# Joint attention stage of a decoder kernel: which scores share a buffer, and where the row maxima are joined

## Chip, cores and metric

One core of one Trainium2 chip runs the whole program. The metric is the device time of one execution in microseconds (us). The chip's engines are TensorE (PE; its weight loads are listed apart as PEld), VectorE (DVE), ScalarE (ACT), GpSimd (POOL) and SyncE (SP), which issues the DMAs.

## What is computed

The reference is a two-layer decoder on 16 x 128 = 2048 rows of 256 features. Each layer has a self-attention, a cross-attention and a feed-forward network, each followed by a layer norm on the sum with its input. The change lies in layer 0's cross-attention, which has 16 heads of 16 dimensions and fake-quantised operands and weights; its 2048 queries see 2048 keys:

```python
q = jnp.transpose((x @ Wq + bq) * scale, ...)      # per head
q = _fq_sym(q, axis=-1)      # round(q / s) * s with s = max|q| / 127
k = _fq_sym(k, axis=-1)
v = _fq_sym(v, axis=2)
attn = jnp.einsum('bhqd,bhkd->bhqk', q, k)
attn = jax.nn.softmax(attn.astype(jnp.float32), axis=-1)
attn = _fq_unsigned(attn, axis=-1)     # round(a / s) * s with s = max(a) / 255
out = jnp.einsum('bhqk,bhkd->bhqd', attn, v)
return out @ Wp + bp
```

The layer norm and layer 0's feed-forward network (silu(gate) * up, then down, 1024 wide) follow. Since the largest softmax weight of a row is exp(0) over the sum, the quantised weight is round(255 * exp(score - max)): the kernel writes exp(score - max + ln 255) as an 8-bit integer, and needs for it the maximum over all 2048 keys of a row.

## The kernel before, in words

The program runs layer 0's self-attention, then the joint stage (L0 cross-attention together with L0's feed-forward network), then layer 1. Only the joint stage is touched.

**Steps.** A step is one tile of 128 queries (`u` of a pair `gp` of tiles) and one pair of heads (`i`): 8 pairs of tiles x 8 pairs of heads x 2 tiles = 128 steps, n = 0 to 127. Sixteen steps that share `gp` are called a group here; they are numbered r0 to r15 in it. A step has two parts, `part` 0 and 1, and `at = 2 * n + part`. Nine more steps at the end drain the pipeline.

**Scores** (`scores`, L781; matmuls at L788). A score buffer `s` has 2 x 512 float32 columns[...], and there are two such buffers. A part takes two of them. Keys and queries are held with 64 rows a head (48 of them in use: three bfloat16 parts of 16 dimensions), so the two heads of a pair lie on rows 0 to 63 and 64 to 127. Before the change a buffer holds the same 512 keys of both heads; the quarters of the 2048 keys come in order.

**Scaling** (`scaled`, L791; L795). One DVE instruction a head and quarter multiplies 128 x 512 scores by the query's scale `qs` into the tile `e` in SBUF and takes the maximum along the row. From the second quarter on it begins with the maximum so far (a second scalar operand, `smx`), so that the fourth quarter's maximum is that of the row. `e` has four buffers, two a step.

**Exponent and weights** (`exponent`, L808; L810 and `weights8`, L812; L819). ACT turns the two maxima of a step into `snl` = ln 255 - max, and a step later takes exp(e + snl) of 128 x 2048 elements to 8 bits, once for each head.

**Turning and spreading** (`words_T`, L828; `words_out`, L834; `spread`, L840). PE transposes the 8-bit weights as 32-bit words, four 128 x 128 blocks into a PSUM tile `aTp` (L831). A copy takes it to SBUF (`at`, L837): in part 0 on DVE, in part 1 on ACT. POOL widens it to bfloat16 (L841). Then PE multiplies with the values (`context`, L854), 32 output rows a head.

**Order.** The scheduler keeps the written order on PE, DVE, ACT and POOL (`manual_schedule`). Work with no place of its own goes through `later(at, engine, f)` and `due(at, engine)`: queries of the next pair of tiles, the division by the softmax sums (L882), the output projection (L887, L890), norm statistics (L136, L137), and the feed-forward network: a `unit` (L922 matmuls; L940 tanh and L941 copy on ACT; L944, L947 and L948 on POOL) in r0, r1, r2, r9, r11, r12, r14 and r15, from the second group on, and its down projection (L957) in r3 to r5 from the third. In every part PE's order is: score buffer 1 of the part, some context, the transposes, score buffer 0 of the next part, more context, feed-forward.

Of the kernel before, what the change touches and what calls it, by code (L numbers as in the profile page):

```python
# [18 lines left out]
F32 = mybir.dt.float32  # L19
# [3 lines left out]
AF = mybir.ActivationFunctionType  # L23
ALU = mybir.AluOpType
AX = mybir.AxisListType
PSUM = bass.MemoryType.PSUM

P = 128
# [4 lines left out]
G = 512  # L33
# [15 lines left out]
def decoder(ctx: ExitStack, tc: tile.TileContext, w: dict, out: bass.AP):  # L49
    nc = tc.nc  # L50

    const = ctx.enter_context(tc.tile_pool(name="const", bufs=1))
    stat = ctx.enter_context(tc.tile_pool(name="stat", bufs=4))
# [156 lines left out]
    with ExitStack() as ph:  # L210
        pool = ph.enter_context(tc.tile_pool(name="l0a", bufs=1))
# [12 lines left out]
        wts, bias = {}, {}  # L224
        for hg in range(4):
            cols = slice(hg * G, (hg + 1) * G)
            for nm in ("Wlk", "Wq", "Wlv"):
                t = wts[nm, hg] = pool.tile([P, 2, G], F32, name=f"{nm}_{hg}")
# [8 lines left out]
            t = wts["Wo", hg] = pool.tile([P, 4, HID], F32, name=f"Wo_{hg}")  # L237
# [284 lines left out]
        states, cks = {}, {}  # L522
# [4 lines left out]
        with tc.manual_schedule(engines={mybir.EngineType.PE}):  # L527
# [4 lines left out]
            for n in range(len(steps) + 6):  # L532
# [34 lines left out]
                g, r = (n + 10) // 16, (n + 10) % 16  # L567
# [21 lines left out]
    with ExitStack() as ph:  # L589
# [173 lines left out]
        nc.sync.dma_start(out=wp2, in_=w["L0_xattn_Wp"].rearrange("(c p) n -> p c n", p=P))  # L763
        for c in range(2):
            nc.gpsimd.tensor_scalar(wp2[:, c], wp2[:, c], sv[:, c : c + 1], 1.0, ALU.mult, ALU.mult)
        ln255 = pool.tile([P, 1], F32, name="ln255")
        nc.gpsimd.memset(ln255, math.log(255.0))

        wk = ph.enter_context(tc.tile_pool(name="l0x_k", bufs=2))
        ps = ph.enter_context(tc.tile_pool(name="l0x_ps", bufs=1, space=PSUM))  # L770
# [7 lines left out]
            ssum = stat.tile([P, 2, 16], F32, tag="ssum", name="ssum", bufs=3)  # L778
            groups[gp] = ([], ssum)

        def scores(gp, i, u, half, c):  # L781

            t = 2 * gp + u
            s = ps.tile([P, 2, G], F32, tag="s", name="s", bufs=2)
            at = (2 * half + c) * G
            for hh in range(2):
                r = slice(64 * hh, 64 * hh + 64)
                nc.tensor.matmul(s[:, hh, :], lhsT=qT[t % 4][r, i, :], rhs=kT[r, i, at : at + G], start=True, stop=True)  # L788
            return s

        def scaled(gp, i, u, half, c, st, s):  # L791

            quarter = 2 * half + c
            for hh in range(2):
                nc.vector.tensor_scalar(  # L795
                    st["e"][hh][:, half, c * G : (c + 1) * G],
                    s[:, hh, :],
                    qs[2 * gp + u][:, 2 * i + hh : 2 * i + hh + 1],
                    None if quarter == 0 else st["mx"][:, quarter - 1, hh : hh + 1],
                    ALU.mult,  # L800
                    ALU.max,
                    accum_out=st["mx"][:, quarter, hh : hh + 1],
                )

        def head(i, hh):
            return 4 * (i // 2) + i % 2 + 2 * hh

        def exponent(st):  # L808
            st["nm"] = stat.tile([P, 2], F32, tag="snl", name="snl")
            nc.scalar.activation(st["nm"], st["mx"][:, 3, :], AF.Identity, bias=ln255, scale=-1.0)  # L810

        def weights8(gp, i, u, hh, st):  # L812

# [20 lines left out]
        def words_out(hh, st, pt, copy):  # L834

            at = wk.tile([P, 4, P], F32, tag="at", name="at", bufs=3)
            copy(at.bitcast(U16), pt.bitcast(U16))  # L837
            st["at"][hh] = at
# [137 lines left out]
        def due(at, engine):  # L976
            for f, args in put_off.pop((at, engine), []):
                f(*args)
# [135 lines left out]
        with tc.manual_schedule(engines=set(ordered)):  # L1114
            for n in range(len(steps) + 9):
                now = steps[n] if n < len(steps) else None
                if now is not None:
                    if n % 16 == 0:
                        group(n // 16)
                    if n < NB:  # L1120
                        nc.gpsimd.tensor_tensor(xs[n], xs[n], bp, ALU.add)
                    states[n] = {
                        "e": [wk.tile([P, 2, 2 * G], F32, tag="e", name="e", bufs=4) for _ in range(2)],
                        "mx": stat.tile([P, 4, 2], F32, tag="smx", name="smx"),
                        "a": [],
                        "at": {},
                    }
                for part in range(2):
                    at = 2 * n + part
                    if now is not None:  # L1130
                        if at == 0:
                            waiting = scores(*now, 0, 0)
                        scaled(*now, part, 0, states[n], waiting)
                        scaled(*now, part, 1, states[n], scores(*now, part, 1))
                    due(at, "DVE")
                    m = n - 2 + part
                    due(at, "PE")
                    for hh in range(2):

                        q = n - 3 if (n - 3) % 2 == 1 else n - 4  # L1140
                        turn = (2 * (n - q) + part, hh)

                        if hh == 1 and 0 <= m < len(steps):
                            pt = words_T(1 - part, states[m])
                        if hh == 1 and at + 1 < 2 * len(steps):
                            waiting = scores(*steps[(at + 1) // 2], (at + 1) % 2, 0)
                        if 0 <= q < len(steps) and turn in turns:
                            gp, i, _ = steps[q]
                            if turn == (7, 0) and i % 4 == 0:
                                os[gp, i // 4] = ps.tile([P, 2 * P], F32, tag="o", name="o")  # L1150
                            o = os[gp, i // 4]
                            context(i, range(*turns[turn]), aTs[gp, i], o)
                            if turn == (9, 1):
                                aTs.pop((gp, i))
                                if i % 4 == 3:
                                    later(
                                        at + 1,
                                        "ACT first",
                                        nc.scalar.copy,
                                        ot[:, i // 4],  # L1160
                                        os.pop((gp, i // 4)).rearrange("p (u q) -> p u q", u=2),
                                    )
                                if i == 7 and gp < LAST:
                                    later(at, "DVE last", sums, gp)
                                    for u in range(2):
                                        later(at + 1, "POOL", by_dim, gp, u)
                    if part == 1:
                        unit(n, 1, at)
                    due(at, "ACT first")

                    if 0 <= n - 1 < len(steps):
                        weights8(*steps[n - 1], part, states[n - 1])
                    if 0 <= m < len(steps):
                        words_out(1 - part, states[m], pt, nc.scalar.copy if part else nc.vector.tensor_copy)
                    due(at, "ACT")
                    if 0 <= n - 2 < len(steps):
                        gp, i, u = steps[n - 2]
                        if part == 0 and u == 0:
                            aTs[gp, i] = wk.tile([P, NB, 2, 2 * P], BF16, tag="aT", name="aT")
                        due(at, "POOL first")  # L1180
                        spread(u, part, states[n - 2], aTs[gp, i])
                    due(at, "POOL first")
                    due(at, "POOL")
                    if now is not None and part == 1:
                        exponent(states[n])
                    due(at, "DVE last")
                    if (n, part) == (len(steps), 1):
                        later(at + 1, "DVE", sums, LAST)
                        for u in range(2):
                            later(at + 2, "POOL", by_dim, LAST, u)  # L1190
                    if n < len(steps):
                        pair_work(n, bool(part))
                    else:
                        tail_work(n, bool(part))
                if n == len(steps) + 3:
                    ffn_load_all()
                states.pop(n - 3, None)
            assert not put_off, put_off

            for i in range(NI):  # L1200
                for n in range(2):
                    ffn_gate(LAST, i, n, "s")
                th, gu = ffn_tiles(LAST, i, tail=True)
                ffn_out(LAST, th, gu)
                ffn_sigmoid(th, nc.vector)
                ffn_mult(LAST, i, th, gu, nc.vector)
            exp_tables()
            for u in range(2):
                ffn_put_out(LAST, range(NI * u, NI * u + NI), 0, "s")
                due(1, "DVE")  # L1210
            due(1, "POOL")
            due(2, "POOL first")
# [498 lines left out]
```

## Time and profile before

| what | value |
|---|---|
| median of 3 runs | 2860.21 us (2859.89 to 2861.86) |
| profiled execution, its own time | 2860.04 us |
| its span, first to last instruction | 2858.3 us |
| joint stage, first to last scaling (L795) | 879.6 to 1750.0 us |
| busy, whole span | PE 2607.9, DVE 2071.4, ACT 1584.7, POOL 1238.4 us |
| busy, 880 to 1750 us | DVE 854, PE 740, ACT 732, POOL 638 us |
| mean granted PE clock | 0.962 |

How to read it: the profile lists for each engine the instructions with their start and length. A group's line gives the source line, the engine, the operation, output and inputs by the program's names and shapes, the count, then the busy time, the mean length in ns, and the idle time of that engine just before them with what ended it. A window's line gives the stretch, its length, the busy time (and count of instructions) of PE, PEld, DVE, ACT and POOL, the granted clock of PE, the DMA share and GB/s. Busy lengths of neighbouring instructions overlap, so what an instruction costs its engine is read from start to start in the timeline.

### The profile page before, as it was taken

The page shows a single profiled execution, that of the slowest core. Times are in us where ns is not written, and L with a number is a line of the kernel's source. Part 1 is how long each engine was busy: PE and PEld are TensorE (multiplying, and loading weights), DVE is VectorE, ACT ScalarE, POOL GpSimd, SP SyncE. Part 2 cuts the span into 40 slices and gives each one's busy share as a digit, 9 for nine tenths or more (in the row PEclk, how much of TensorE's full clock was granted, in tenths as well). Part 3 has the DMA queues.
Part 4 walks back from the last instruction along what each step waited for, and adds up shares of the span by engine and source line. Part 5 has one row for each costly group of instructions (what it writes and reads, how often), then busy time and mean ns, then how long its engine had stood idle before and what let it go on. Part 6 is the DMA issues. An engine that isn't in the chain of part 4 may idle for free. (4 is left out here: it accounts for less than half of the span.)

```text
span 2858.3 us, 44732 instructions
## 1 busy us (share of the span) xinstructions
PE 2607.9 (91%) x15989; PEld 1620.2 (57%) x16020; DVE 2071.4 (72%) x5525; ACT 1584.7 (55%) x2858; POOL 1238.4 (43%) x1390
## 2 busy tenths in 40 slices
PE   6999999999976788888889888899988899999998
PEld 3677777777753344444445444566655555665646
DVE  5677877877759999999999995577877763233232
ACT  3455555555536888878888885455555442222120
POOL 5644544444446667768777776323322200000000
PEclk9999999999996889999999999999999999999999
DMA  8000000000010000000000001400010012111120
GB/s 239 2 1 1 1 1 1 1 1 1 1 38 10 1 12 20 25 12 25 23 12 27 19 16 50 145 2 1 2 49 12 6 38 67 36 53 48 41 62 13
DMA packets 85006, 79.69 MB, mean 28 GB/s; under 512 B 19728, under 2 KB 66288, under 8 KB 84272
## 3 DMA queue, kind: packets, MB, share of 16 engines
q1 hardware_dynamic: 83520, 73.41, 8.5%
q0 software_dynamic: 1264, 3.42, 0.5%
q8 instruction: 127, 2.08, 0.3%
q14 instruction: 95, 0.78, 0.1%
HBM read 74.57 MB, written 2.23 MB: 27 GB/s over the span
## 5 line engine op out<-in xcount | busy, mean ns | idle before, releaser
L795 DVE TENSOR_SCALAR_CACHE_REDUCE e<-s,qs,smx 128x512 f32<-128x512 f32 x768 | 581.5, 806 | 12.3 <-PE s L788 11.7
L841 POOL CAST aT<-at 128x2048 bf16<-128x2048 uint8 x256 | 482.9, 1891 | 194.7 <-DVE at L837 133.4
L819 ACT ACTIVATE a<-e,snl 128x2048 uint8<-128x2048 f32 x256 | 510.8, 1998 | 2.8
L788 PE MATMUL s<-kT,qT 64*128 64x512 bf16 x1024 | 216.4, 416 | 99.6 <-DVE e L795 97.1
L1623 DVE TENSOR_TENSOR h<-h,up 128x512 f32<-128x512 f32 (+1 forms) x100 | 68.8, 688 | 192.6 <-PE up L1619 191.3
L854 PE MATMUL o<-aT,vq 128*32 128x256 bf16 x2048 | 193.7, 294 | 0.0
L831 PE MATMUL aTp<-ident,a 128*128 128x128 f32 x1024 | 181.7, 304 | 13.0 <-ACT a L819 12.6
L788 PEld LDWEIGHTS <-qT 64*128 64x128 bf16 x1024 | 61.9, 94 | 228.6 <-issue 227.5
L795 DVE TENSOR_SCALAR_CACHE_REDUCE e<-s,qs 128x512 f32<-128x512 f32 x256 | 179.6, 739 | 4.8 <-PE s L788 4.8
L1622 ACT ACTIVATE h<-gate 128x512 f32<-128x512 f32 (+1 forms) x100 | 59.7, 597 | 220.5 <-PE gate L1619 220.3
L1619 PE MATMUL gate<-xT,w_L_ffn_w1g 128*128 128x512 f32 x352 | 167.7, 595 | 0.0
L837 ACT COPY at<-aTp 128x1024 uint16<-128x1024 uint16 x128 | 128.4, 1003 | 69.6 <-PE aTp L831 64.7
L1619 PE MATMUL up<-xT,w_L_ffn_w1u 128*128 128x512 f32 x352 | 165.4, 592 | 0.0
L1333 DVE TENSOR_REDUCE amx<-sc 128x8 f32<-128x1024 f32 x96 | 116.7, 1215 | 62.2 <-PE sc L1324 62.0
L831 PEld LDWEIGHTS aTp<-ident,a 128*128 128x128 f32 x1024 | 116.6, 150 | 77.2 <-issue 35.8
L1650 PE MATMUL py<-w_L_ffn_w2T,h 128*128 128x256 f32 x704 | 154.6, 379 | 0.0
L1336 ACT ACTIVATE pr<-pr 128x1024 f32<-128x1024 f32 x96 | 101.6, 1059 | 88.3 <-DVE pr L1335 88.3
L1345 ACT COPY prT<-tp 128x512 f32<-128x512 f32 x192 | 104.2, 583 | 76.8 <-PE tp L1344 76.4
L1650 PEld LDWEIGHTS py<-w_L_ffn_w2T,h 128*128 128x128 f32 x704 | 133.7, 190 | 18.3
L922 PE MATMUL gu<-xT,wgu 128*128 128x256 f32 x448 | 128.4, 410 | 1.8 <-ACT gu_s L941 1.7
L854 PEld LDWEIGHTS <-vq 128*32 128x32 bf16 x2048 | 72.7, 98 | 100.0 <-issue 94.5
L443 ACT ACTIVATE pls<-sc,lm,rms_rs 128x128 f32<-128x128 f32 x256 | 113.7, 453 | 21.7 <-DVE lm L439 21.7
(319 smaller groups left out, 5961.7 us busy)
## 6 DMA issues: line engine op xcount, KB each, us to landing
wgu<-in_L_ffn_gu SPq DMA_DIRECT2D x112, 128.0 KB
sh<-share SPq DMA_DIRECT2D x32, 256.0 KB
sh<-share SPq DMA_DIRECT2D x16, 224.0 KB
sh<-share SPq DMA_DIRECT2D x16, 192.0 KB
w_L_ffn_w1g<-in_L_ffn_w1g SPq DMA_DIRECT2D x1, 2816.0 KB
w_L_ffn_w1u<-in_L_ffn_w1u SPq DMA_DIRECT2D x1, 2816.0 KB
w_L_ffn_w2T<-in_L_ffn_w2T SPq DMA_DIRECT2D x1, 2816.0 KB
sh<-share SPq DMA_DIRECT2D x16, 160.0 KB
```

What stands on the lines that cost most here:

```text
L443: nc.scalar.activation(pls[:, h, :], by_head[:, h // 2, h % 2, NC4:NK], AF.Exp, bias=nm[:, h : h + 1], scale=rq[:, h : h + 1], accum_out=s ...
L788: nc.tensor.matmul(s[:, hh, :], lhsT=qT[t % 4][r, i, :], rhs=kT[r, i, at : at + G], start=True, stop=True)
L795: nc.vector.tensor_scalar(st["e"][hh][:, half, c * G : (c + 1) * G], s[:, hh, :], qs[2 * gp + u][:, 2 * i + hh : 2 * i + hh + 1], None if ...
L819: nc.scalar.activation(a.bitcast(U8), st["e"][hh].rearrange("p a b -> p (a b)"), AF.Exp, bias=st["nm"][:, hh : hh + 1], accum_out=groups[g ...
L831: nc.tensor.transpose(pt[:, b, :], st["a"][hh][:, b * P : (b + 1) * P], ident)
L837: copy(at.bitcast(U16), pt.bitcast(U16))
L841: nc.gpsimd.tensor_copy(aT[:, :, hh, u * P : (u + 1) * P].rearrange("p (b j) q -> p b j q", j=4), st["at"].pop(hh).bitcast(U8).rearrange(" ...
L854: nc.tensor.matmul(o[r : r + 32], lhsT=vq[:, n, h // 2, h % 2 : h % 2 + 2].rearrange("p w d -> p (w d)"), rhs=aT[:, n, hh], start=n == 0 a ...
L922: nc.tensor.matmul(ffn_ps[q][:, n, :], lhsT=wt[:, k, :], rhs=xT[q // 2][:, k, at], start=k == 0, stop=k == 1)
L1333: nc.vector.tensor_reduce(mx, sc, AX.X, ALU.max)
L1619: nc.tensor.matmul(pp[:rows], lhsT=wt[:, k, :], rhs=xT[g][:, k, :], start=k == 0, stop=k == 1)
L1650: nc.tensor.matmul(py, lhsT=h[:rows, i4 * P : (i4 + 1) * P], rhs=wt, start=n == 0, stop=n == len(parts) - 1)
```

## The change

Three things change. First, in the first half of a step (part 0, keys 0 to 1023) a score buffer holds one head's 1024 keys in place of both heads' 512, and one DVE instruction scales all 1024; in the second half both heads share a buffer as before. Second, no scaling begins with an earlier maximum: a step leaves three maxima a head, which DVE joins at the end of the step with a reduction, and DVE also forms ln 255 - max, which ACT did; this comes right behind the last scaling in the order. Third, the copy of transposed words is on DVE only in part 0 of even steps (`at % 4 == 0`), otherwise on ACT.

```diff
-        ln255 = pool.tile([P, 1], F32, name="ln255")
-        nc.gpsimd.memset(ln255, math.log(255.0))
...
-        def scores(gp, i, u, half, c):
+        def scores(gp, i, u, half, x):
             t = 2 * gp + u
             s = ps.tile([P, 2, G], F32, tag="s", name="s", bufs=2)
-            at = (2 * half + c) * G
-            for hh in range(2):
+            for j in range(2):
+                hh, c = (x, j) if half == 0 else (j, 2 + x)
                 r = slice(64 * hh, 64 * hh + 64)
-                nc.tensor.matmul(s[:, hh, :], lhsT=qT[t % 4][r, i, :], rhs=kT[r, i, at : at + G], start=True, stop=True)
+                nc.tensor.matmul(
+                    s[:, j, :], lhsT=qT[t % 4][r, i, :], rhs=kT[r, i, c * G : (c + 1) * G], start=True, stop=True
+                )
             return s
-        def scaled(gp, i, u, half, c, st, s):
-            quarter = 2 * half + c
-            for hh in range(2):
+        def scaled(gp, i, u, half, x, st, s):
+            blocks = [(x, s.rearrange("p a b -> p (a b)"), st["e"][x][:, 0, :])]
+            if half == 1:
+                blocks = [(hh, s[:, hh, :], st["e"][hh][:, 1, x * G : (x + 1) * G]) for hh in range(2)]
+            for hh, src, dst in blocks:
                 nc.vector.tensor_scalar(
-                    st["e"][hh][:, half, c * G : (c + 1) * G],
-                    s[:, hh, :],
+                    dst,
+                    src,
                     qs[2 * gp + u][:, 2 * i + hh : 2 * i + hh + 1],
-                    None if quarter == 0 else st["mx"][:, quarter - 1, hh : hh + 1],
+                    None,
                     ALU.mult,
                     ALU.max,
-                    accum_out=st["mx"][:, quarter, hh : hh + 1],
+                    accum_out=st["mx"][:, half + half * x, hh : hh + 1],
                 )
         def exponent(st):
+            m = stat.tile([P, 2], F32, tag="smm", name="smm")
+            nc.vector.tensor_reduce(m, st["mx"].rearrange("p q h -> p h q"), AX.X, ALU.max)
             st["nm"] = stat.tile([P, 2], F32, tag="snl", name="snl")
-            nc.scalar.activation(st["nm"], st["mx"][:, 3, :], AF.Identity, bias=ln255, scale=-1.0)
+            nc.vector.tensor_scalar(st["nm"], m, -1.0, math.log(255.0), ALU.mult, ALU.add)
...
-                        "mx": stat.tile([P, 4, 2], F32, tag="smx", name="smx"),
+                        "mx": stat.tile([P, 3, 2], F32, tag="smx", name="smx"),
...
                         scaled(*now, part, 1, states[n], scores(*now, part, 1))
+                        if part == 1:
+                            exponent(states[n])
...
-                        words_out(1 - part, states[m], pt, nc.scalar.copy if part else nc.vector.tensor_copy)
+                        words_out(1 - part, states[m], pt, nc.vector.tensor_copy if at % 4 == 0 else nc.scalar.copy)
...
-                    if now is not None and part == 1:
-                        exponent(states[n])
```

## The prediction

> **What bounds the kernel now.** I read the 40 slices first (VectorE, DVE, at 9 tenths only where line 795 runs), then the costliest groups, then the windows of the joint stage, step by step. The stage's 128 steps run from 879.6 us (first instruction of L795) to 1750.0 us (its last): 870 of the 2858.3 us span. Eight groups of 16 steps take 103, 107, 111, 110, 109, 110, 111 and 109 us. Everything that the change touches lies there.
>
> The costliest groups, columns as on the page (count, then busy us, mean ns, idle before):
>
> ```profile
> L795 DVE TENSOR_SCALAR_CACHE_REDUCE e<-s,qs,smx 128x512 f32<-128x512 f32 x768 | 581.5, 806 | 12.3 <-PE s L788 11.7
> L788 PE MATMUL s<-kT,qT 64*128 64x512 bf16 x1024 | 216.4, 416 | 99.6 <-DVE e L795 97.1
> L795 DVE TENSOR_SCALAR_CACHE_REDUCE e<-s,qs 128x512 f32<-128x512 f32 x256 | 179.6, 739 | 4.8 <-PE s L788 4.8
> L837 DVE COPY at<-aTp 128x1024 uint16<-128x1024 uint16 x128 | 87.6, 684 | 1.3 <-PE aTp L831 1.3
> ```
>
> DVE hardly ever waits for scores (16.5 us in 870); TensorE (PE) waits 97 us for DVE to free a score buffer. So DVE sets the pace. But by how much? The windows of the fourth group, one per step (us, then busy PE, PEld, DVE, ACT, POOL, then PE clock), show it; I number its steps r0 to r15:
>
> ```profile
> 1206.72:1213.06 6.34, 6.34 (x46) 3.44 (x47) 6.34 (x18) 6.31 (x11) 5.47 (x6) 1.00 0.16 44
> ...
> 1241.09:1248.02 6.93, 4.21 (x31) 1.94 (x29) 6.93 (x18) 4.80 (x5) 6.50 (x9) 0.84 0.00 0
> 1248.02:1257.67 9.65, 9.09 (x52) 4.64 (x50) 8.31 (x26) 6.27 (x8) 3.27 (x2) 0.76 0.01 3
> 1257.67:1264.01 6.34, 3.88 (x23) 1.68 (x22) 6.34 (x19) 4.39 (x5) 5.90 (x8) 0.64 0.00 0
> 1264.01:1270.95 6.94, 6.94 (x49) 3.51 (x46) 6.42 (x20) 5.77 (x8) 3.89 (x3) 0.84 0.07 19
> ...
> sum 110.31, PE 97.06 PEld 52.45 DVE 107.94 ACT 93.39 POOL 84.00; mean PE 6.07 PEld 3.28 DVE 6.75 ACT 5.84 POOL 5.25
> ```
>
> DVE is busy 107.9 of 110.3 us, but r1 (first row) has PE and ACT full as well, and in r7 and r9 PE, at half clock for part of the time, already makes the step longer than DVE's busy time. The bound is DVE's by a small margin in the odd steps and by a large one in r6, r8 and r14.
>
> PE in r1, back to back (start us, length, what):
>
> ```profile
> 1207.63 0.39 PE L788 MATMUL s<-kT,qT 64*128 64x512 bf16 x2
> 1207.95 0.39 PE L854 MATMUL o<-aT,vq 128*32 128x256 bf16 x4
> 1208.28 0.66 PE L831 MATMUL aTp<-ident,a 128*128 128x128 f32 x4
> 1208.86 0.39 PE L788 MATMUL s<-kT,qT 64*128 64x512 bf16 x2
> 1209.18 0.51 PE L854 MATMUL o<-aT,vq 128*32 128x256 bf16 x6
> 1209.62 1.13 PE L922 MATMUL gu<-xT,wgu 128*128 128x256 f32 x4
> ```
>
> Both score matmuls of a buffer end within 0.39 us, no longer than one alone: they lie on different halves of the array's rows and run together (starts 4 ns apart). The next step's first score starts at 1213.73: PE needs 6.10 us for a step to which DVE gives 6.34.
>
> **The change, part by part.** DVE first. From its timeline, start to start: a scaling instruction with only the query scale takes 0.67 us, one that also takes the running maximum 0.73, the copy 0.61. A step is 2 x 0.67 + 6 x 0.73 + 0.61 = 6.33, the 6.34 of the plain windows.
>
> After, a step has two scalings of 1024 and four of 512, all without the running maximum. 512 more elements cost 0.53 us (the reductions of 128x512 and 128x1024 take 683 and 1215 ns), so a long one takes 1.20 start to start. The copy stays in even steps only. The join X: the last accumulator read and its wait about 0.12 (83 ns, plus the 35 ns that each dependent DVE pair here shows), the reduction 0.17 (rnm 169 ns; np_mv, six in and two out, 182), 35 ns, then 0.08 start to start for the small scalar operation (sums, L469). X = 0.40; at least 0.25 (the reduction of svs took 102), at most 0.55. It runs in DVE's queue ahead of the postponed work and the next step's first scaling, which wait that long; it can't gain. Even step: 2 x 1.20 + 4 x 0.67 + 0.61 + 0.40 = 6.09, 0.24 less. Odd: 5.48, 0.85 less. Mean 0.55, over 128 steps 70 us of DVE time.
>
> Here a rule speaks against the saving. The Trainium skill, VectorE: DVE Perf Modes, "The DRAIN you can't avoid", says that a semaphore between DVE operations costs nothing extra, since the pipe empties anyway. Six of the eight scalings now wait for an earlier maximum. By the rule they would save nothing by losing that, and the mean saving would be 0.55 - 6 x 0.063 = 0.17 us, 22 us in all. The rows show 0.73 against 0.67 for equal tiles (whether the wait or the second scalar operand costs it, they don't tell); the change takes both away, so I take the rows.
>
> PE: in the first half of a step a buffer's two matmuls are now of one head, on the same rows, so they follow each other. Pairs of o matmuls follow at 0.11 for 256 columns, so 512 take 0.21; the weight load hides behind the first matmul, as in the gu chain (0.22 apart). Two buffers a step: +0.43 us at full clock, +0.85 at half; at least zero (they can't overlap better than now), at most 0.62 if the second load (94 ns) isn't hidden. The skill's TensorE: Matmul & The Clock Gate, "Back-to-back issue gap", gives about 131 ns a matmul for a load-matmul stream at 512 columns, by which the cost would be 0.26; nothing here runs that fast, so 0.43. It lies on the path wherever PE has no slack.
>
> ACT: the 128 snl operations leave (0.34 each, start to start), 64 copies come (1.0 each, 0.9 start to start): even steps -0.34, odd +0.56, so its 93.4 us become about 95. The copy in odd first halves waits on PE's transposes between two exponentials, so the second exponential and whatever needs it slip 0.9 us; the tiles e of scaled scores are two steps deep, which covers it while ACT is under about 2 us late. The maximum now comes 0.4 us after the last scaling, as it did through ACT (0.37). The memset that goes, POOL's spreads and SP's weight loads keep their cost and place: nothing.
>
> **The sum.** For the fourth group, DVE per step after: 6.1, 5.5, 6.1, 5.7, 7.0, 6.6, 6.7, 7.5, 6.1, 5.6, 6.9, 5.6, 6.0, 6.3, 6.3, 5.4, together 99.2 (its busy time less 0.24 or 0.85). PE's work per step, by its timeline from score to score less its idle, was 5.5, 6.1, 5.6, 6.5, 6.4, 7.5, 4.2, 8.7, 4.5, 7.0, 5.6, 5.7, 6.2, 6.2, 4.7, 6.7; with 0.43 added (0.7 in r7, r8 and r9, partly at half clock): 6.0, 6.5, 6.0, 7.0, 6.8, 7.9, 4.6, 9.4, 5.2, 7.7, 6.0, 6.2, 6.6, 6.6, 5.1, 7.1, together 104.7. The larger of the two in each step adds up to 110.1. After r6, r8 and r14 PE enters a buffer ahead, about 0.8 each: -2.4. PE's short waits for ACT and DVE (4.6 us in this group: 1.9 for exponentials, the rest for x, qa, rows) now partly lie in steps that PE bounds: +2. PE is denser in r6 to r8, so I take off a third of the 3.4 us that the half clock costs r7 and r9: -1.1. That leaves about 108.6 to 109.3: a gain of 1 us a group, 6 in groups three to eight. The first group has no feed-forward work; DVE gains 0.24 and 0.85 in turn and PE at half clock gives back some 2.5 us: -6. The second is like it up to r8: -3.5. In all -15.5 against the profiled run's 2860.04 (span 2858.3), which is 0.2 us from the median of 2860.21: **2845**. The gain of 70 goes mostly to PE, which is late next in every odd step.
>
> **The rivals.** PE hides its extra: if the half clock vanishes with the denser PE, or most stalls do, DVE's full 70 us come through: 2790, halfway 2810. For it: r6, r8 and r14 have slack. Against it: r1's full PE row. Chance 0.12.
>
> Slower: PE's extra matmuls fall on steps without slack. Credit for lead gone, waits for exponentials doubled (ACT has 6.3 of 6.34 in r1 to r3 and more copies), half clock as now: 110.1 + 2 + 1.5 = 113.6 a group, less 0.7 of smoothing, 112.9: +2.6, six times, less 9.5: +6, so 2866; with unhidden loads (0.19 more a step, 3 us a group) up to 2880. It decides once PE's work and waits pass 110.3 a group, that is from 0.4 us of unhidden stalls a step. Chance 0.28.
>
> Break-even: both meet within 0.2% (5.7 us, about what a measurement of this kernel can tell from no change): 2857. Chance 0.16. That the change doesn't do what it says I exclude: the instruction order of the built kernel has two long and four short scalings, a reduction and a scalar operation each step.
>
> **How the numbers follow.** The likeliest case, 2828 to 2854, holds 0.44; with the first rival faster is 0.54 (a little of the case ends above 2854.5), same 0.17, slower 0.29. The range reaches 2816 to 2872.
>
> **What would show it.** Long scalings at 1.20 start to start, short ones at 0.67, X at 0.4; score pairs of first halves 0.6 us long; DVE's waits for scores up from 16 us to over 60; PE's for DVE down from 97 to under 60; odd steps at about 6.5 with PE full, even at 6.1. I am wrong if DVE stays full (then near 2790), or if PE waits for ACT's exponentials over 0.5 us a step (then slower).

## The result, and the profile after

The changed kernel takes 2922.58 us (median of 4 runs, 2921.71 to 2922.69) against 2860.05 (4 runs, 2857.31 to 2861.86): 62.5 us longer, ratio 1.022 [1.020, 1.024]. The profiled execution took 2921.71 us, its span is 2920.0. The joint stage, first to last scaling, grew from 870.4 to 926.3 us; the other 6 us of the span lie before and behind it. The groups of 16 steps went from 103, 107, 111, 110, 109, 110, 111 and 109 us to 107, 109, 118, 120, 120, 120, 120 and 115.

The costliest groups of the changed kernel, the ones that answer to those shown of before (count, busy us, mean ns, idle before and who ended it):

```profile
L798 DVE TENSOR_SCALAR_CACHE_REDUCE e<-s,qs 128x512 f32<-128x512 f32 (+1 forms) x768 | 674.3, 921 | 82.2 <-PE s L787 80.3
L824 ACT ACTIVATE a<-e,snl 128x2048 uint8<-128x2048 f32 x256 | 513.4, 2010 | 55.9 <-DVE snl L815 55.6
L787 PE MATMUL s<-kT,qT 64*128 64x512 bf16 x1024 | 280.6, 422 | 74.5 <-DVE e L798 71.0
```

DVE's scalings fell from 761 busy us to 678 (each the sum of its two groups), and DVE now waits 80 us for scores where it waited 16.5: so far as foretold. But in the middle line ACT's exponentials wait 55.6 us for `snl`, the operand that DVE now makes. Before, ACT made `snl` itself and waited there for DVE's maxima:

```profile
ACT snl L810 <- DVE e L795: 33.2, 34, 6.8
```

So that wait is not new, but it is 22 us longer. The groups of DVE in the joint stage, each shape apart, say why:

```profile
L798 DVE TENSOR_SCALAR_CACHE_REDUCE e<-s,qs 128x512 f32<-128x512 f32 x512 | 356.8, 746 | 32.0 <-PE s L787 31.5
L798 DVE TENSOR_SCALAR_CACHE_REDUCE e<-s,qs 128x1024 f32<-128x1024 f32 x256 | 321.2, 1273 | 50.2 <-PE s L787 48.8 <-ACT at L842 0.4
L815 DVE TENSOR_SCALAR snl<-smm 128x2 f32<-128x2 f32 x128 | 74.8, 584 | 4.5
...
L813 DVE TENSOR_REDUCE smm<-smx 128x2 f32<-128x6 f32 x128 | 20.4, 159 | 4.4
```

The reduction of six maxima to two takes 159 ns. The scalar operation behind it, on two elements a row, takes 584 ns on average, 74.8 us in all. The line for its tile gives shortest, median and longest:

```profile
L815 DVE TENSOR_SCALAR snl<-smm x128: 169/458/1887, 887.2 to 1808.3; 128x2 f32<-128x2 f32 x128
```

An operation whose size is fixed and whose time goes from 169 to 1887 ns is waiting inside. For what, two timelines show, of DVE and then of POOL, between r6 and r7 of the fourth group (start us, length us):

```profile
1267.89 0.16 DVE L813 TENSOR_REDUCE smm<-smx 128x2 f32<-128x6 f32 x1
1268.09 1.73 DVE L815 TENSOR_SCALAR snl<-smm 128x2 f32<-128x2 f32 x1
1269.73 1.27 DVE L798 TENSOR_SCALAR_CACHE_REDUCE e<-s,qs 128x1024 f32<-128x1024 f32 x1
```

```profile
1264.23 5.56 POOL L846 CAST aT<-at 128x2048 bf16<-128x2048 uint8 x3
```

POOL's third cast ends at 1264.23 + 5.56 = 1269.79; the scalar operation ends at 1269.82. Over all 128: the 39 that start with POOL idle take 169 to 172 ns, every one. Of the 61 that start during a cast (918 ns on average) 55 end 21 to 25 ns after that cast's end; of the 28 that start during other POOL work (L952, L953, L1126) 22 end 23 to 26 ns after its end. The remaining twelve started in the last 82 ns of POOL's instruction and took 169 to 172 ns, as with POOL idle. All 128 wait for one semaphore, which only DVE sets, so the program ties none of them to POOL; the operation holds DVE's queue, with the next step's first scaling behind it, until POOL's instruction is over. The Trainium skill, SBUF — State Buffer, "SBUF: two separate sides", has a rule of this shape: DVE and GpSimd share a port pair, which a DVE instruction in a two-port mode takes as an exclusive lock, and the loser blocks fully. VectorE: DVE Perf Modes, "The perf-mode tier table", lists a float32 `tensor_scalar` in SBUF in such a mode, but reductions and float32 operations that read PSUM not. The numbers agree: the scalings read PSUM and the reduction is a reduction, and neither waited (158 to 161 ns for every one of the 128 reductions).

The kernel before shows the same outside the joint stage. A plain scalar operation on 128x256 from SBUF to SBUF (L719) takes 293 ns with POOL idle and 495 to 726 in the 13 cases that start while POOL runs; the reductions of L385 stay at 623 to 689 whether POOL runs or not. Operations on two SBUF tiles (L293) stretch too: 409 to 417 ns with POOL idle, up to 1106 otherwise.

The second part shows in PE's timeline of r1, the step the prediction took as its example:

```profile
1221.25 0.60 PE L787 MATMUL s<-kT,qT 64*128 64x512 bf16 x2
1221.78 0.50 PE L859 MATMUL o<-aT,vq 128*32 128x256 bf16 x6
...
1223.28 0.60 PE L787 MATMUL s<-kT,qT 64*128 64x512 bf16 x2
...
1224.73 0.39 PE L787 MATMUL s<-kT,qT 64*128 64x512 bf16 x2
1225.05 0.51 PE L859 MATMUL o<-aT,vq 128*32 128x256 bf16 x6
...
1227.78 0.60 PE L787 MATMUL s<-kT,qT 64*128 64x512 bf16 x2
```

A pair of score matmuls of one head takes 0.60 us, a pair of two heads 0.39 as before, and r1 lasts 6.53 us from its first score to the next step's, as was worked out (6.10 + 0.43). The windows of the fourth group (r1, r4, r6, r7 and the sum; us, then busy PE, PEld, DVE, ACT, POOL, then PE clock):

```profile
1222.76:1229.09 6.33, 6.33 (x45) 3.09 (x44) 5.93 (x16) 6.33 (x9) 4.15 (x4) 1.00 0.16 45
...
1241.98:1251.59 9.61, 7.13 (x41) 4.04 (x41) 8.67 (x20) 6.83 (x8) 7.46 (x7) 0.97 0.01 2
...
1261.48:1269.73 8.25, 6.26 (x43) 3.04 (x42) 8.18 (x18) 4.27 (x5) 7.80 (x9) 1.00 0.01 2
1269.73:1277.20 7.47, 5.71 (x40) 2.84 (x39) 7.26 (x21) 6.82 (x7) 1.96 (x2) 1.00 0.00 0
...
sum 119.52, PE 105.46 PEld 53.23 DVE 106.14 ACT 97.05 POOL 83.57; mean PE 6.59 PEld 3.33 DVE 6.63 ACT 6.07 POOL 5.22
```

r1 (6.33 from scaling to scaling) has PE full, as foretold. r4 and r6 have an operation of 1.89 and 1.73 us in them; in r6 DVE is full for that reason, and POOL nearly so. DVE's busy time, foretold as 99.2, is 106.1, and no engine is full over the group's 119.5 us.

### The profile page after: what moved, and what is told of

Read it like the earlier page. It is cut to its first block, busy times and chain, and to the rows that moved or that the text cites. A ratio compares the mean times of both kernels' runs of the same rounds, so it can differ in the third digit from the quotient of the medians.

```text
span 2920.0 us, 44132 instructions
## 1 busy us (share of the span) xinstructions
PE 2685.5 (92%) x16020; PEld 1626.7 (56%) x16020; DVE 2054.1 (70%) x5205; ACT 1611.3 (55%) x2794; POOL 1237.0 (42%) x1389
## 5 line engine op out<-in xcount | busy, mean ns | idle before, releaser
L798 DVE TENSOR_SCALAR_CACHE_REDUCE e<-s,qs 128x512 f32<-128x512 f32 (+1 forms) x768 | 674.3, 921 | 82.2 <-PE s L787 80.3
L824 ACT ACTIVATE a<-e,snl 128x2048 uint8<-128x2048 f32 x256 | 513.4, 2010 | 55.9 <-DVE snl L815 55.6
L787 PE MATMUL s<-kT,qT 64*128 64x512 bf16 x1024 | 280.6, 422 | 74.5 <-DVE e L798 71.0
L842 ACT COPY at<-aTp 128x1024 uint16<-128x1024 uint16 x192 | 193.9, 1010 | 69.2 <-PE aTp L836 68.2
L373 PE MATMUL proj<-Wlk,xT 128*128 128x512 f32 x256 | 122.3, 600 | 2.9 <-ACT raw_Wlv L399 1.7
```

The source lines that it names most:

```text
L787: nc.tensor.matmul(s[:, j, :], lhsT=qT[t % 4][r, i, :], rhs=kT[r, i, c * G : (c + 1) * G], start=True, stop=True)
L798: nc.vector.tensor_scalar(dst, src, qs[2 * gp + u][:, 2 * i + hh : 2 * i + hh + 1], None, ALU.mult, ALU.max, accum_out=st["mx"][:, half + ...
L824: nc.scalar.activation(a.bitcast(U8), st["e"][hh].rearrange("p a b -> p (a b)"), AF.Exp, bias=st["nm"][:, hh : hh + 1], accum_out=groups[g ...
```

## The experiments

The theories. **P**: the scalar operation on `snl` waits for POOL's running instruction and so stops DVE's queue, about 50 us. **S**: PE, with its matmuls of a pair one after the other, is what costs the 62 us; in its smaller form, **S2**, it costs only what is left once the scalar operation no longer waits. **A**: the copies that went to ACT make the weights late. Each ratio below is to the kernel before on the same chip, with its 95% interval. In four kernels, named below, the exponent lacks ln 255, so their weights and outputs are other numbers, though the same instructions run on the same shapes. Code is shown in cuts; `...` marks what is left out. The kernels before had medians of 2858.92 us (first four runs), 2858.44 (next four) and 2860.09 (last three).

**The change with the exponent on ACT.** DVE keeps the reduction; ACT forms ln 255 - max from it, at the old place.

```diff
         def exponent(st):
             m = stat.tile([P, 2], F32, tag="smm", name="smm")
             nc.vector.tensor_reduce(m, st["mx"].rearrange("p q h -> p h q"), AX.X, ALU.max)
+            st["m"] = m
+
+        def exponent_act(st):
             st["nm"] = stat.tile([P, 2], F32, tag="snl", name="snl")
-            nc.vector.tensor_scalar(st["nm"], m, -1.0, math.log(255.0), ALU.mult, ALU.add)
+            nc.scalar.activation(st["nm"], st["m"], AF.Identity, bias=ln255, scale=-1.0)
...
+                    if now is not None and part == 1:
+                        exponent_act(states[n])
```

> The changed kernel, but ln 255 - max is again formed on ACT, at its old place; the reduction stays on DVE. Theory P (the small scalar operation on DVE waits for POOL's running instruction: 74.8 us in 128 instructions instead of 21.8 at 170 ns each): those 53 us of DVE time go, and what PE waited for with them; 2850 to 2875. Rival S (the score pairs that PE now runs one after the other cost the time): PE's work is unchanged, so 2905 to 2922. Rival A (more copies on ACT): ACT gets 0.34 us a step more, so no better than 2922.

Measured 2878.68 us, 1.0068 [1.0053, 1.0083]. 44 us come back for one small operation moved; S had nearly none of that. A little more stays than P gave (3.7 us over its range), and DVE waits 107.6 us for scores: PE's pairs are still there.

**The kernel before with only the exponent on DVE**, right behind the last scaling, in the same form of instruction:

```diff
-            nc.scalar.activation(st["nm"], st["mx"][:, 3, :], AF.Identity, bias=ln255, scale=-1.0)
+            nc.vector.tensor_scalar(st["nm"], st["mx"][:, 3, :], -1.0, math.log(255.0), ALU.mult, ALU.add)
...
+                        if part == 1:
+                            exponent(states[n])
...
-                    if now is not None and part == 1:
-                        exponent(states[n])
```

> The kernel before, with one edit: ln 255 - max is formed by a small scalar operation on DVE right behind the last scaling, not on ACT. Theory P: the operation waits for POOL some 0.4 us on average in a stage that DVE bounds, plus 0.1 us of its own, so 2860 + 128 x 0.5 = 2924, at least 2900. Rivals S and A: 0.1 us a step, at most 2875.

Measured 2946.77 us, 1.0307 [1.0290, 1.0325]. One small operation a step, nothing else changed, and the kernel is 88 us longer; it alone more than makes up the result. The tile's line in this kernel:

```profile
L808 DVE TENSOR_SCALAR snl<-smx x128: 168/512/1894, 885.9 to 1836.4; 128x2 f32<-128x2 f32 x128
```

The same spread, up to the 1.89 us that a POOL cast takes. It costs more here than in the changed kernel: 83 us of DVE's queue (652 ns on average, 584 there), and all of it shows in the kernel's time. DVE waits only 17 us for scores here, so there was little slack to take it up.

**The layout alone.** Before, with one head's keys in a buffer in the first half; running maxima, exponent on ACT and copies as they were.

```diff
-                    None if quarter == 0 else st["mx"][:, quarter - 1, hh : hh + 1],
+                    None if half == 0 else st["mx"][:, half + half * x - 1, hh : hh + 1],
...
```

> The kernel before with the new contents of the score buffers alone: a head's 1024 keys in the first half, running maxima kept in the second, exponent on ACT, copies as before. DVE saves 0.41 us a step, PE's pairs of the first half run one after the other (0.43 us a step more). Theory P: within 15 us of before, 2845 to 2875. Rival S: most of the loss is here, 2895 to 2925.

Measured 2880.26 us (2869.9 to 2882.2), 1.0066 [1.0047, 1.0085]: between the two. The long scalings save DVE time in every step, and still the layout by itself costs 20 us. S is wrong as the account of 62 us, and right in kind.

**The copies alone.**

```diff
-                        words_out(1 - part, states[m], pt, nc.scalar.copy if part else nc.vector.tensor_copy)
+                        words_out(1 - part, states[m], pt, nc.vector.tensor_copy if at % 4 == 0 else nc.scalar.copy)
```

> The kernel before with the copies moved alone: on DVE in the first part of even steps, otherwise on ACT. DVE saves 0.3 us a step on average, ACT gets 0.95 more in odd steps. Theory P: 2840 to 2862. Rival A: ACT or the transposes that wait for it become late, 2875 to 2900.

Measured 2863.18 us, 1.0018 [1.0010, 1.0025]. It is 1 us over P's range and far below A's. DVE has 0.6 us less to do in every odd step, and the kernel is 4 us longer all the same: DVE's waits for scores rise from 16.5 to 38.2 us, and the weight loads of PE's transposes wait 43.0 us for ACT's exponentials in place of 26.2.

**The change with the scalar operation in another form**: the same operation with an accumulator output, the form that the scalings have. In this form the second scalar is only what the accumulator starts from (the kernel before hands on its running maximum that way), so ln 255 is left out of the exponent here, and in the next three kernels.

```diff
-            nc.vector.tensor_scalar(st["nm"], m, -1.0, math.log(255.0), ALU.mult, ALU.add)
+            dump = stat.tile([P, 1], F32, tag="snd", name="snd")
+            nc.vector.tensor_scalar(st["nm"], m, -1.0, math.log(255.0), ALU.mult, ALU.add, accum_out=dump)
```

> The changed kernel with one edit: the small scalar operation on DVE also writes an accumulator, which makes it the operation that the scalings are (TENSOR_SCALAR_CACHE_REDUCE), at the same place, on the same two columns. Theory P (the plain form waits for POOL's running instruction, this one doesn't): the operation takes about 0.2 us every time, POOL is as busy as before; 2865 to 2885, near the 2878.7 of the run with the exponent on ACT. Rival: the place or the dependence on the reduction makes the wait, whatever the form; 2915 to 2925.

Measured 2871.93 us, 1.0059 [1.0031, 1.0087]: 51 us less than the change, at the same place in the queue and with the same tiles. The tile's line:

```profile
L816 DVE TENSOR_SCALAR_CACHE_REDUCE snl<-smm x128: 154/155/157, 885.9 to 1759.1; 128x2 f32<-128x2 f32 x128
```

All 128 take the same 155 ns, with POOL as busy as ever. So neither the place nor the tiles nor the count makes the wait, but the form of the instruction.

**That kernel with its pairs on different rows.** The second 512 columns of a first-half buffer get the other head's scores in place of this head's, so the work and the shapes are the same and the scores are mixed between heads.

```diff
-                hh, c = (x, j) if half == 0 else (j, 2 + x)
+                hh, c = (j, x) if half == 0 else (j, 2 + x)
```

> As e5_other_form, but the two matmuls of a first-half buffer read different row halves again (the second 512 columns hold the other head's scores, so this part of the computation is changed; every instruction, size and wait stays). Theory S2 (what remains of the loss without the wait for POOL is PE's pairs running one after the other, 0.43 us a step): PE's work falls back by 0.43 us a step; 20 us or more faster than e5_other_form, 2835 to 2858. Rival (longer scalings hold a buffer longer, or the copies on ACT are the cause): within 6 us of e5_other_form.

Measured 2841.83 us, 0.9938 [0.9923, 0.9953]. 30 us go with the order of the pairs: that is S2.

**That kernel (pairs as in the change) with the copies as before.**

```diff
-                        words_out(1 - part, states[m], pt, nc.vector.tensor_copy if at % 4 == 0 else nc.scalar.copy)
+                        words_out(1 - part, states[m], pt, nc.scalar.copy if part else nc.vector.tensor_copy)
```

> As e5_other_form, but the copies of transposed words as before, on DVE in every first part. DVE gets 0.6 us more in odd steps, ACT 0.95 less. Rival A (the copies on ACT delay the exponentials): 10 us or more faster than e5_other_form. Theory S2: PE bounds the odd steps, DVE has room there; within 8 us of e5_other_form.

Measured 2874.83 us, 1.0092 [1.0055, 1.0129], by the medians 2.9 us above the kernel with the change's copies. Of seven executions four took 2873.0 to 2874.8 us and three 2900.4 to 2902.0; of six with the change's copies five took 2866.7 to 2874.0 and one 2892.9. What sets the longer ones apart isn't known. A needed this kernel to be 10 us or more faster; no execution of it is faster than the other's median, so A falls.

**The kernel before with the exponent on DVE, in the other form.**

```diff
-            nc.vector.tensor_scalar(st["nm"], st["mx"][:, 3, :], -1.0, math.log(255.0), ALU.mult, ALU.add)
+            nc.vector.tensor_scalar(st["nm"], st["mx"][:, 3, :], -1.0, math.log(255.0), ALU.mult, ALU.add, accum_out=dump)
```

> The kernel before with the exponent on DVE behind the last scaling, as in e2_exponent_on_dve (2946.8), but in the accumulating form. Theory P: no wait for POOL, only the operation's own 0.2 to 0.3 us a step in a stage that DVE bounds, 26 to 38 us at most: 2865 to 2897. Rival (any form at this place waits): near 2947.

Measured 2885.74 us, 1.0092 [1.0077, 1.0107]: 61 us less than the same kernel with the plain form. What is left over before, 27 us or 0.21 us a step, is what remains when the operation no longer waits: it and its accumulator read stand in a queue that has hardly any slack.

**The whole change with the join mended.** The reduction negates, and the scalar operation adds ln 255 as its first scalar, with an accumulator output that nobody reads: all of the computation is there again.

```diff
-            nc.vector.tensor_reduce(m, st["mx"].rearrange("p q h -> p h q"), AX.X, ALU.max)
+            nc.vector.tensor_reduce(m, st["mx"].rearrange("p q h -> p h q"), AX.X, ALU.max, negate=True)
...
-            nc.vector.tensor_scalar(st["nm"], m, -1.0, math.log(255.0), ALU.mult, ALU.add)
+            nc.vector.tensor_scalar(st["nm"], m, math.log(255.0), None, ALU.add, ALU.max, accum_out=dump)
```

> The changed kernel with the join mended: the reduction negates, and ln 255 is added by an operation with an accumulator (the form that did not wait for POOL in e5_other_form), so that the whole computation is as in the reference. Theory P + S2: as e5_other_form, 2866 to 2880. Rival: the 44 to 50 us between this and the changed kernel do not come from the form; then above 2900.

Measured 2873.32 us, 1.0045 [1.0033, 1.0058]. This is the kernel that the prediction thought it was pricing: the small operation costs what it was given, and the kernel is still 13 us slower than before. Its waits (in all, times, longest), and its windows of r0, r1, r7, r8, r9, r15 and the sum of the fourth group:

```profile
DVE e L798 <- PE s L787: 86.5, 132, 4.1
...
PE s L787 <- DVE e L798: 53.1, 78, 1.5
```

```profile
1201.86:1208.80 6.94, 6.34 (x43) 3.22 (x40) 6.13 (x16) 6.26 (x7) 6.45 (x7) 1.00 0.13 38
1208.80:1215.16 6.36, 6.36 (x44) 3.09 (x44) 5.62 (x17) 6.36 (x9) 4.19 (x4) 1.00 0.16 44
...
1251.28:1258.77 7.49, 7.17 (x49) 3.31 (x48) 7.28 (x23) 6.84 (x7) 3.51 (x2) 1.00 0.01 2
1258.77:1264.89 6.12, 3.96 (x20) 1.56 (x21) 6.05 (x17) 4.26 (x5) 5.67 (x8) 0.72 0.00 0
1264.89:1274.18 9.29, 9.29 (x50) 4.26 (x47) 5.71 (x18) 6.39 (x7) 4.09 (x3) 0.64 0.05 14
...
1308.56:1314.84 6.28, 6.11 (x48) 3.02 (x48) 5.50 (x17) 5.99 (x9) 5.98 (x7) 1.00 0.14 42
sum 112.98, PE 102.92 PEld 52.34 DVE 99.51 ACT 96.96 POOL 83.69; mean PE 6.43 PEld 3.27 DVE 6.22 ACT 6.06 POOL 5.23
```

DVE's 99.5 is the 99.2 that was foretold. The group's 113.0 is not the 109, but the slower rival's 112.9. In r9 PE is full for 9.29 us at a mean clock of 0.64.

**The whole change with the join mended and the rows packed anew**, so that a buffer of one head's 1024 keys still takes its matmuls from both halves of the rows. For keys 0 to 1023, `kT` holds a head's first 512 keys on rows 0 to 63 and its next 512 on rows 64 to 127; a second copy of a tile's queries, `qS`, has the halves exchanged (two DMAs a tile). To make room, `a` has three buffers in place of four, and the feed-forward weights two in place of three.

```diff
             for j in range(2):
-                hh, c = (x, j) if half == 0 else (j, 2 + x)
-                r = slice(64 * hh, 64 * hh + 64)
+                c = x if half == 0 else 2 + x
+                r = slice(64 * j, 64 * j + 64)
+                q = qS[t % 2] if half == 0 and x != j else qT[t % 4]
...
```

> As e8_join_mended, with a head's keys 0 to 511 on rows 0 to 63 and its keys 512 to 1023 on rows 64 to 127, and a second copy of the queries with the heads' rows exchanged (two DMAs a tile of queries), so that both matmuls of every score buffer lie on different rows and still hold one head's 1024 keys; to make room, tiles a have 3 buffers, feed-forward weights 2 with a load less ahead. Theory S2: PE's work a step as before, 2838 to 2852, faster than before the change. Rival (the buffers that were taken away, or the exchange of rows, cost what is won): 2860 or more.

Measured 2846.05 us, 0.9949 [0.9937, 0.9962]: all of the computation is done, and it is 14 us faster than before and 27 faster than the mended join. The stage itself is 32 us shorter (849.3 against 881.5). In the profiled executions 8 us of that go again outside it: 1 before the stage, where the first keys and queries are packed, and 7 behind it, which was not followed up. The sum of its fourth group, and one of its waits:

```profile
sum 108.27, PE 94.76 PEld 51.42 DVE 99.32 ACT 96.47 POOL 83.56; mean PE 5.92 PEld 3.21 DVE 6.21 ACT 6.03 POOL 5.22
```

```profile
DVE e L830 <- PE s L819: 42.2, 68, 1.2
```

DVE's work is the mended kernel's to 0.2 us; PE has 8.2 us less, and DVE waits half as long for scores.

**The join and the copies without the layout.** Before, with no running maximum in any scaling, the mended join over four quarters behind the last, and the change's copies.

```diff
-                    None if quarter == 0 else st["mx"][:, quarter - 1, hh : hh + 1],
+                    None,
...
```

> The kernel before with the score buffers as before, but without running maxima: four maxima a head joined at the end by the negating reduction and the operation with an accumulator, copies as in the changed kernel. DVE: 8 x 0.67 + 0.3 + 0.45 = 6.1 us a step on average, 0.2 less than before; PE's pairs together. Theory S2 (the rest of the loss was PE's pairs): no loss, 2835 to 2862. Rival (joining the maxima costs by its place or latency, whatever the layout): 2870 or more.

Measured 2850.18 us, 0.9962 [0.9948, 0.9975]: 10 us faster than before, by the two parts of the change that remain. From this side the layout costs 2873.3 - 2850.2 = 23 us; alone it cost 20, and by the packing it gives back 27. Its scalings and its join, by shape:

```profile
L793 DVE TENSOR_SCALAR_CACHE_REDUCE e<-s,qs 128x512 f32<-128x512 f32 x1024 | 706.4, 744 | 32.5 <-PE s L786 29.4 <-ACT a L820 0.3
...
L808 DVE TENSOR_REDUCE smm<-smx 128x2 f32<-128x8 f32 x128 | 20.6, 161 | 4.4
L811 DVE TENSOR_SCALAR_CACHE_REDUCE snl<-smm 128x2 f32<-128x2 f32 x128 | 19.8, 155 | 4.4
```

## Why the prediction was wrong

The sign was wrong, and the result lies 78 us above the forecast and 51 above the range. Of the 78, 49 go with one term of the sum, which the mended join puts right (2922.6 - 2873.3); 28 are left in the mended kernel (2873.3 - 2845) and are the rest of the sum.

**The term that failed: "then 0.08 start to start for the small scalar operation (sums, L469)".** The operation is 0.58 us long on average in place of 0.17, so it takes 0.49 start to start, and the join X came to about 0.81 us in place of 0.40, outside its bounds of 0.25 and 0.55. No term of the bound is a wait for POOL: the prediction took POOL's part in the change as nothing. Two rows of the kernel before had it, one in the very row the term was taken from:

```profile
L469 DVE TENSOR_SCALAR sums<-sums x64: 170/171/717, 51.7 to 799.5; 128x8 f32<-128x8 f32 x64
```

```profile
L665 DVE TENSOR_SCALAR sv<-sv x1: 466/466/466, 836.2 to 836.2; 128x2 f32<-128x2 f32 x1
```

L665 is the same operation on the same shape as the new one, and its 466 ns end 25 ns after a POOL instruction of L716; four of L469's 64 start while POOL runs an instruction, and all four wait for it (717, 690, 259 and 256 ns long, ending 25 to 28 ns after it). The median, 171, comes from the 60 that met none. The stage that the operation moved into has POOL at 84 us of 110 and in pieces of 1.89 us. With POOL busy for a share of 0.76 of the time, a start at random in a piece, and every piece taken as long as a cast, an estimate of the wait is 0.76 x 1.89 / 2 = 0.72 us; measured 0.41. The estimate is too high, but 0.72 us a step is more than the 0.55 that DVE was to gain, and would have put the change at slower.

**The second failure: the credits in the sum.** The parts of it were right. DVE per group: 99.2 foretold, 99.5 in the mended kernel. PE's pairs: 0.60 us against 0.39, +0.43 us a step, neither the 0.26 nor the 0.62 that were weighed. What failed is "a gain of 1 us a group". The prediction added the larger of two engines' work in each step (110.2 from its rounded steps), took off 3.5 us, 2.4 for the lead that PE gains in slack steps and 1.1 for less half clock, and put 2 us on for PE's waits. In the fourth group of the mended kernel, each came out worse. The credits show in r6 to r9, which take 29.6 us where the larger of the two gives 29.9, and in r14 and r15, 12.5 for 13.4: about 1.2 us, not 3.5. The other ten steps take 3.9 us more than the larger of the two, not 2. Together 110.2 - 1.2 + 3.9 = 112.9; measured is 113.0, forecast was about 109.

Part of the 3.9 lies in r0, r2, r4 and r10, where DVE should have set the pace: there it waits 0.5 to 1.3 us for PE, and the steps take 6.7 to 7.9 us in place of 6.1 to 7.0. In r0 DVE is busy for the 6.1 us foretold, but the step lasts 6.94, and PE is full in r1 after it. The half clock gave next to nothing because it moved: in the fourth group it fell from 13.7 us to 10.2, but onto r9, where PE is full (r7 and r9 took 9.65 and 6.94 us before, 7.49 and 9.29 then). In the whole stage PE ran at half clock for 151 us before and 150 in the mended kernel.

Groups three to eight make up 18 of the 28 us. Another 9 are the first two groups, forecast as 6 and 3.5 us shorter in a sentence each: the first came out 2.1 us shorter, the second 1.6 us longer. Why was not followed up.

**The rivals.** "Slower: PE's extra matmuls fall on steps without slack" is what the mended kernel did: credit for the lead mostly gone, waits about doubled, and its 112.9 for a group against 113.0. That its figure for a group is so close is in part luck, since its waits are a plain doubling and its 0.7 of smoothing a guess; the time, 2866, is 7 us under the 2873 measured. The changed kernel itself went past that rival's end of 2880, by a mechanism that none of the rivals held.

**The signs named ahead.** Long scalings at 1.20 and short ones at 0.67 start to start: right (1269.73 to 1270.93, for one). X at 0.4: wrong, and right once mended. Score pairs of 0.6: right. DVE's waits for scores over 60: right, at 80.3. PE's for DVE under 60: wrong at 71.0, since DVE was held up; 53.1 when mended. Odd steps of about 6.5 with PE full: right in r1 (6.33) and r3 (6.53), wrong in most others. Even ones of 6.1: wrong, also in the mended kernel (r0 takes 6.94). PE waiting for ACT's exponentials over 0.5 us a step, the sign of a slower kernel, did not come: PE and its weight loads wait 29 us for them in the changed kernel, 0.2 us a step, and 40 before. The kernel was slower for another reason.

**The rule that was weighed** ("The DRAIN you can't avoid", of the Trainium skill's VectorE: DVE Perf Modes): the choice of the row over it holds. Scalings that don't begin with an earlier maximum are 744 ns long without the layout, against 806 before, and the join without the layout, of which this is the main saving, gains 10 us beside copies that by themselves gain nothing. Whether the wait or the second scalar operand cost the 62 ns, no run separates.

**What stays open.** That POOL's instruction is what holds the operation rests on the ends of the 89 that start while POOL runs, on the constant 169 to 172 ns of the 39 that don't, and on the form that doesn't wait; no run took POOL's casts away or shortened them. By what part of the chip POOL holds it is told by the rule named above alone; the runs show only when it waits. What decides in which step the half clock falls wasn't settled either, nor why the waits in the other ten steps came to 3.9 us a group.

## What to carry to other kernels

Before a small operation is moved to another engine, look at the spread of that operation's time in the trace, not at its median, and at what other engines run where it goes: shortest 170 and longest 717 ns for one shape is a wait, and it grows with the length of the instructions it waits for. In a queue that sets the pace, the form of an instruction can be worth more than its size: one output more took 49 us out of this kernel. And where the larger of two engines' work is added up step by step, whatever is taken off that sum has to be shown in a row first: here 3.5 us a group were taken off and 1.2 came.

## What the runs showed of the hardware

- A plain DVE scalar operation from SBUF to SBUF on 128x2 float32 took 168 to 172 ns with POOL idle and up to 1894 ns while POOL ran a cast; where it was held up, it ended 21 to 28 ns after POOL's instruction. Nearly the same operation with an accumulator output took 154 to 157 ns always, and a reduction to 128x2 158 to 161: neither waits.
- With an accumulator output, the second scalar is what the accumulator starts from and does not reach the output: the kernel before hands on its running maximum so, and `e` holds the scaled scores alone.
- Two score matmuls of 512 columns on the same 64 rows take 0.60 us, on different halves of the rows 0.39.
